# Shared expert of the last sequences moved behind the expert blocks, a wider ring of row numbers, and a new hand-written order in a one-core decoder layer

## The chip, the core and the metric

The kernel runs on one core of a Trainium2 chip. The core has five engines with an instruction stream each: TensorE (PE; its weight loads are listed apart as PEld), VectorE (DVE), ScalarE (ACT), GpSimd (POOL) and SyncE (SP), which here only issues transfers. Each engine works through its own stream in order, and streams wait for each other by semaphores. Transfers run on 16 DMA engines. The metric is the device time of one launch in microseconds.

## The reference, cut to what matters

A pre-norm decoder layer on 16 sequences of 256 tokens with 256 features, all in f32: attention with 16 heads of 16 features, an additive "cross" term, and a mixture of 16 experts with one shared expert. `ln` is a layer norm.

```python
# attention, after ln twice (the second with weight and bias)
q, k, v = heads(h @ w_q), heads(h @ w_k), heads(h @ w_v)        # rope on q and k
t = 1 + s + 0.5 * s * s            # s = q k^T / 4, a Taylor softmax
x = x + ((t / t.sum(-1)) @ v) @ w_o
# cross: a number per token plus a number per feature column
x = x + (ln(x) @ w_dec)[:, :, None] + (ctx @ w_enc)[:, None, :] + bias
# experts, y = ln(x)
scores = sigmoid(y @ gate_w.T)
topk_w, topk_idx = top_k(scores, 2)              # normalised, times 2.5
routed = sum over the two chosen e of weight * (silu(y @ w_gate[e]) * (y @ w_up[e])) @ w_down[e]
shared = (silu(y @ ws_gate) * (y @ ws_up)) @ ws_down
x = x + routed + shared
```

## The kernel before, in words

**Two phases.** In the first, the 16 sequences go through attention, cross term and routing. In the second, the routed expert work is done in 79 blocks of 128 rows, each block of one expert.

**First phase.** A `Sequence` has some 50 small tasks as methods (`turn_h`, `project`, `rope`, `score`, `square`, `product`, `output`, `decode`, `choose`, `place`, `enlist` and so on), and each task issues the instructions of one engine, mostly. The list `ORDER` (L854) is an order written out by hand: iteration i of the loop at L906 walks it once, and an entry (lag, task) runs that task for sequence i - lag. So tasks of up to eight sequences alternate in each engine's stream; the largest lag is 7, and the loop runs for 16 + 7 iterations. The last iterations, in which there are no new sequences, hold less and less of this work. A sequence ends with its routing: `logits` and `sigmoid` give scores, `choose` takes the top two on VectorE, `count` and `place` work out a row number ("slot") for each choice of a token, and `enlist` (L791) writes each token's normalised row with its weights to these slots of a DRAM table `listed`, in four indirect transfers that POOL issues. Every tile in PSUM of this phase comes from three pools: `p_sc` (two buffers, scores), `p_av` (one) and `p_t` (three, everything else).

**Shared expert.** `Shared` (L809) treats four token tiles (512 tokens) as a unit; there are eight units. `gate_up` is eight TensorE instructions into a `p_sc` buffer, `hidden` is a sigmoid on ACT and two multiplications on VectorE, `down(half)` is four TensorE instructions into a `p_t` buffer, and `add(half)` adds two token tiles to `x_all` on VectorE. The list `DRAIN` (L873) puts these pieces among the entries of the last iterations: (3, 24, 0, "down", 0) runs `down(0)` of unit 0 before entry 24 in iteration 16 + 3. What is left runs after the last iteration.

**Second phase.** `Block` i loads 128 rows of `listed` on SP (nine blocks ahead; the first load waits for all enlistings), `turn` transposes them on TensorE and ACT copies them, `pick` works out on VectorE each row's weight and its row number in the result, an i32 column `dest` from a ring of six buffers (L959), `hidden_product` multiplies by the block's expert (`gu`) and takes Silu on ACT, `weigh` multiplies on VectorE, `turn_hidden` transposes (`th`, copied to `hidT` on VectorE), and `give` (L996) multiplies by the down weights (`eo`), copies to `got` (ACT, six buffers) and writes the rows to a DRAM table `given` at `dest` by an indirect transfer from POOL. Step i of the loop at L1049 runs these stages for blocks i, i - 2, i - 3 and i - 4.

**Sums.** All rows of sequence b are given once block `last`(b) is. At step `last` + 7 `fetch(b)` (L1015) reads the two rows of each of its tokens back on SP, 512 KB, and waits for every `give` issued so far that no earlier fetch has waited for:

```python
ins = nc.sync.dma_start(out=got, in_=given_t[:, ts(b, TT)])
behind(ins, gave)
gave.clear()
```

From four steps later on, one `add` (L1025) a step adds a part of 128 x 256 to `x_all`, and the fourth writes the sequence out on SP:

```python
nc.vector.tensor_tensor(acc, acc, got[:, t, c], ALU.add)
if part == 2 * TT - 1:
    nc.sync.dma_start(out=out_t[:, ts(b, TT)], in_=x_all[:, ts(b, TT)])
```

What has not been added when the loop ends is added behind it (L1079).

Of the kernel before, what the change touches and what calls it, by code (L numbers as in the profile page):

```python
# [51 lines left out]
P = 128  # L52
# [23 lines left out]
def decoder_kernel(  # L76
# [192 lines left out]
    with tc.tile_pool(name="work", bufs=2) as work, tc.tile_pool(  # L269
# [576 lines left out]
        def turn_gate():  # L846
# [5 lines left out]


        ORDER = [  # L854
            (3, "score", 1), (4, "turn_x", 1), (3, "square", 1, 0), (7, "enlist", 1),
            (2, "rope", 1), (4, "normalise", 0), (5, "turn_h3"), (4, "normalise", 1),
            (3, "product", 0), (5, "copy_h3"), (5, "logits"), (0, "load"), (0, "stat"),
            (3, "square", 1, 1), (4, "turn_w"), (0, "experts", 0), (5, "sigmoid"), (1, "turn_h"),
            (1, "encode"), (4, "copy_w"), (5, "choose"), (2, "rope_sum", 1), (1, "copy_h"),
            (3, "score", 2), (4, "output"), (3, "square", 2, 1), (2, "turn_q"), (3, "sum_values"),  # L860
            (4, "add_y"), (3, "square", 2, 0), (3, "copy_vsum"), (3, "turn_vsum"),
            (3, "product", 1), (4, "decode"), (3, "score", 3), (6, "enlist", 0), (2, "copy_q"),
            (2, "turn_k"), (3, "copy_x", 0), (0, "scale"), (5, "count"), (3, "square", 3, 0),
            (1, "project_v"), (4, "scale_dec"), (3, "square", 3, 1), (0, "norm"),
            (3, "product", 2), (2, "copy_k", 0), (0, "experts", 1), (4, "get_enc"), (5, "place"),
            (3, "product", 3), (2, "copy_k", 1), (2, "score", 0), (4, "add_cross"),
            (1, "project", 0), (1, "rope", 0), (4, "norm3"), (3, "copy_x", 1), (1, "copy_v"),
            (1, "rope_sum", 0), (1, "project", 1), (2, "square", 0, 1), (2, "square", 0, 0),
            (3, "turn_x", 0),
        ]  # L870


        DRAIN = [  # L873
            (2, 50, 3, "gate_up"), (2, 62, 0, "gate_up"), (3, 4, 3, "hidden"), (3, 9, 0, "hidden"),
            (3, 24, 0, "down", 0), (3, 30, 0, "add", 0), (3, 35, 5, "gate_up"),
            (3, 47, 3, "down", 1), (3, 49, 3, "down", 0), (3, 51, 5, "hidden"),
            (3, 53, 6, "gate_up"), (3, 54, 1, "gate_up"), (3, 59, 3, "add", 0),
            (3, 60, 3, "add", 1), (3, 61, 6, "hidden"), (3, 64, 5, "down", 0), (4, 5, 5, "add", 0),
            (4, 7, 1, "hidden"), (4, 10, 0, "down", 1), (4, 12, 6, "down", 0),
            (4, 20, 0, "add", 1), (4, 21, 7, "gate_up"), (4, 23, 6, "add", 0),  # L880
            (4, 25, 1, "down", 0), (4, 31, 7, "hidden"), (4, 44, 4, "gate_up"),
            (4, 46, 1, "add", 0), (4, 57, 5, "down", 1), (4, 58, 5, "add", 1),
            (4, 60, 6, "down", 1), (4, 61, 2, "gate_up"), (5, 24, 7, "down", 0),
            (5, 26, 4, "hidden"), (5, 30, 6, "add", 1), (5, 44, 4, "down", 0),
            (5, 45, 2, "hidden"), (5, 50, 4, "down", 1), (5, 63, 7, "add", 0), (6, 9, 4, "add", 0),
            (6, 12, 4, "add", 1), (6, 18, 2, "down", 0), (6, 32, 1, "down", 1),
            (7, 9, 2, "add", 0), (7, 21, 2, "down", 1), (7, 27, 7, "down", 1),
            (7, 33, 2, "add", 1), (7, 38, 7, "add", 1), (7, 57, 1, "add", 1),
        ]
        first = Sequence(0)  # L890
        first.stat()
# [35 lines left out]
    with tc.tile_pool(name="ew", bufs=3) as ew, tc.tile_pool(  # L927
# [12 lines left out]
        class Block:  # L940
# [14 lines left out]
            def pick(self):  # L955

                code, own = self.rows[:, D + 2 : D + 3], codes[:, self.i : self.i + 1]
                self.weight = ew.tile([P, 1], F32, tag="weight", name="weight", bufs=4)
                self.dest = ew.tile([P, 1], I32, tag="dest", name="dest", bufs=6)  # L959
                nc.vector.scalar_tensor_tensor(  # L960
                    self.weight, code, own, self.rows[:, D : D + 1], ALU.is_equal, ALU.mult
                )
                nc.vector.scalar_tensor_tensor(
                    self.dest, code, own, self.rows[:, D + 3 : D + 4], ALU.is_equal, ALU.add
                )

                nc.vector.tensor_tensor(
                    self.weight, self.weight, self.rows[:, D + 1 : D + 2], ALU.max
                )
# [26 lines left out]
            def give(self):  # L996
                eo = p_e.tile([P, D], F32, tag="eo", name="eo")
                nc.tensor.matmul(  # L998
                    eo, lhsT=self.hidT,
                    rhs=wd_sb[:, ds(self.e, 1)].rearrange("m a d -> m (a d)"),  # L1000
                    start=True, stop=True,
                )
                got = ew.tile([P, D], F32, tag="got", name="got", bufs=6)
                nc.scalar.copy(got, eo)  # L1004
                ins = nc.gpsimd.indirect_dma_start(  # L1005
                    out=given,
                    out_offset=bass.IndirectOffsetOnAxis(
                        ap=self.dest, axis=0
                    ),
                    in_=got, in_offset=None,  # L1010
                    bounds_check=2 * NT * P - 1, oob_is_err=False,
                )
                gave.append(apart(ins, "given"))

        def fetch(b):  # L1015

            got = ew.tile([P, TT, 2, D], F32, tag="sum", name="sum")
            ins = nc.sync.dma_start(out=got, in_=given_t[:, ts(b, TT)])

            tc.add_to_no_dep_group("given", ins.ins)  # L1020
            behind(ins, gave)
            gave.clear()
            return got

        def add(b, got, part):  # L1025

            t, c = divmod(part, 2)
            acc = x_all[:, b * TT + t]
            nc.vector.tensor_tensor(acc, acc, got[:, t, c], ALU.add)
            if part == 2 * TT - 1:  # L1030
                nc.sync.dma_start(out=out_t[:, ts(b, TT)], in_=x_all[:, ts(b, TT)])

        AHEAD, LANDED, FETCHED = 9, 3, 4
        due = {}
        for b in range(B):
            last = min(NB, ((b + 1) * 2 * TT * P + E * (P - 1)) // P) - 1
            step = last + 4 + LANDED  # L1040
            if due:
                step = max(step, max(due) + 1)
            due[step] = b
# [2 lines left out]
        codes = block_codes()  # L1046
        blocks = [Block(i) for i in range(AHEAD)]
        expert, adds = [], []
        for i in range(max(due) + 1):  # L1049

            if i < NB and i % 4 == 0:
# [8 lines left out]
                blocks[i - 2].hidden_product(expert[i - 2])  # L1060
            if 3 <= i < NB + 3:
                blocks[i - 3].turn_hidden()
            if 4 <= i < NB + 4:
                blocks[i - 4].give()
            if i < NB:
# [10 lines left out]
                    adds.append((i + FETCHED + part, due[i], got, part))  # L1076
            if i + AHEAD < NB:
                blocks.append(Block(i + AHEAD))
        for _, b, got, part in adds:  # L1079
            add(b, got, part)  # L1080
        order.close()


# [30 lines left out]
```

## Time and profile before

| what | us |
|---|---|
| median of 3 runs (548.63 to 550.35) | 549.69 |
| the profiled execution | 552.59 |
| its span, first to last instruction | 550.8 |
| `gate_up` of all shared units on TensorE, 64 instructions, mean 598 ns | 29.2 busy |
| `down` of all shared units, 64 instructions, mean 385 ns | 15.7 busy |
| `given` writes, 79 issues by POOL, mean 987 ns | 78.0 busy |
| sums added on VectorE, 64 instructions, mean 420 ns | 26.6 busy |

Times in a trace are counted from the first instruction of the profiled execution. A row of instructions names line, engine and operation, what it writes and reads, and how often; "busy" is its time in total. TensorE work is pipelined, so its instructions overlap: eight pieces of `gate_up` take 3.43 us in the chain of work, though each lasts 0.6. Idle time before a group is put down to the instruction whose end released it. The chain of work that ended last is followed back from the last instruction.

The first block of the second phase has its rows transposed at 392.96 us, the last `gu` starts at 534.42, and the last indirect write leaves POOL at 539.23.

### The profile page before, as it was taken

The numbers are of one execution on the slowest core, as the hardware profiler recorded it, in microseconds if no ns is written. First come the engines' busy times: TensorE is split into PE (matmuls) and PEld (weight loads), VectorE is DVE, ScalarE is ACT, GpSimd is POOL, SyncE is SP. The second block draws the span as 40 slices with busy tenths as digits, with TensorE's granted clock in tenths as the row PEclk, the third lists the DMA queues.
The fourth block names the chain that finished last, engine by engine and source line by source line (L and its number), as shares of the span: only waits on it lengthen the run. The fifth ranks groups of instructions, "written<-read, shape, count | busy, mean of one in ns | idle before, by whom it ended". The sixth has DMA issues, their size and how long they took to land.

```text
span 550.8 us, 13145 instructions
## 1 busy us (share of the span) xinstructions
PE 506.6 (92%) x4299; PEld 348.0 (63%) x4299; DVE 400.5 (73%) x1723; ACT 307.6 (56%) x651; POOL 309.3 (56%) x496
## 2 busy tenths in 40 slices
PE   2899999999999999999999988999799999889880
PEld 1455676676666666667667654556588878677760
DVE  6534588899988989888888767898555566566663
ACT  3276686676676686676677674211255545445440
POOL 5743556577668668668665643544056555555541
PEclk9799999999999999999999999999899999999996
DMA  6974741241342242232001101101555377777734
GB/s 184 292 239 135 235 151 47 86 146 55 95 145 74 83 135 84 84 99 69 21 32 52 51 21 36 45 29 69 168 163 160 107 252 233 269 258 216 218 110 162
DMA packets 62066, 70.36 MB, mean 128 GB/s; under 512 B 7452, under 2 KB 53421, under 8 KB 62000
## 3 DMA queue, kind: packets, MB, share of 16 engines
q1 hardware_dynamic: 54592, 51.69, 31.0%
q0 software_dynamic: 6864, 17.06, 8.5%
q8 instruction: 35, 0.57, 0.4%
q10 hardware_dynamic: 544, 0.79, 0.4%
q14 instruction: 31, 0.25, 0.2%
HBM read 37.57 MB, written 33.89 MB: 130 GB/s over the span
## 4 chain that ended last, share of the span: by engine, by line
PE 78%; DMA 9%; DVE 5%; ACT 3%; issue 2%; POOL 2%; SPq 0%; POOLq 0%; ACTq 0%; DVEq 0%
PE sc L554 11%; PE av L574 10%; PE pq L458 10%; PE gu L975 8%; DMA given<-got,dest 7%; PE py L627 6%; PE pv L506 5%; PE shared_ps L818 5%; PE eo L998 4%; PE tp_h L438 3%; PE xt_ps L599 3%; PE shared_eo L834 2%; PE tp_e L951 2%; PE tp_k L438 2%; DMA sum<-given 2%
## 5 line engine op out<-in xcount | busy, mean ns | idle before, releaser
L564 ACT ACTIVATE a<-sc 128x1024 f32<-128x1024 f32 x128 | 126.3, 1034 | 52.3 <-PE sc L554 49.8
L1005 POOL DMA_INDIRECT given<-got,dest x79 | 78.0, 987 | 78.3 <-ACT rowsT L953 71.2
L975 PE MATMUL gu<-wgu_sb,rowsT 128*128 x316 | 83.1, 386 | 0.6 <-ACT rowsT L953 0.3
L793 POOL DMA_INDIRECT listed<-h,slots x64 | 65.3, 1021 | 20.7 <-issue 20.4
L554 PE MATMUL sc<-qT,kT 32*128 32x256 f32 x1024 | 76.0, 402 | 0.8 <-ACT a L564 0.8
L289 POOL TENSOR_SCALAR rs<-mv 128x2 f32<-128x2 f32 x48 | 11.5, 240 | 98.1 <-DVE mv L283 96.8
L574 PE MATMUL av<-a,vaug 128*32 128x256 f32 x1024 | 65.4, 382 | 0.0
L554 PEld LDWEIGHTS sc<-qT,kT 32*128 32x128 f32 x1024 | 48.2, 185 | 21.7 <-issue 12.7
L458 PE MATMUL pq<-wqkv,hT 128*128 128x512 f32 x128 | 59.1, 604 | 0.0
L975 PEld LDWEIGHTS gu<-wgu_sb,rowsT 128*128 128x128 f32 x316 | 54.7, 193 | 5.7 <-ACT rowsT L953 0.6
L290 POOL TENSOR_TENSOR rs<-rs,neg_half 128x2 f32<-128x2 f32 x64 | 48.8, 763 | 5.3
L480 POOL TENSOR_TENSOR qkr<-rot,m 128x512 f32<-128x512 f32 x32 | 41.1, 1286 | 16.1 <-DVE m L474 15.8
L1004 ACT COPY got<-eo 128x256 f32<-128x256 f32 x79 | 29.4, 373 | 34.1 <-PE eo L998 21.8
L998 PE MATMUL eo<-wd_sb,hidT 128*128 x158 | 47.7, 383 | 0.0
L574 PEld LDWEIGHTS av<-a,vaug 128*32 128x32 f32 x1024 | 29.0, 109 | 21.9 <-issue 4.9
L585 ACT ACTIVATE xs<-av,vsum 128x256 f32<-128x256 f32 x64 | 26.9, 471 | 27.5 <-PE av L574 20.6
L994 DVE COPY hidT<-th 128x128 f32<-128x128 f32 x79 | 22.7, 288 | 26.1 <-PE th L992 20.7
L981 ACT ACTIVATE hid<-gu 128x128 f32<-128x128 f32 x79 | 22.0, 278 | 35.1 <-PE gu L975 18.0
L468 DVE TENSOR_TENSOR rot<-pq,cosf 128x512 f32<-128x512 f32 x32 | 22.0, 686 | 26.3 <-PE pq L458 25.9
L458 PEld LDWEIGHTS pq<-wqkv,hT 128*128 128x128 f32 x128 | 23.1, 189 | 28.0 <-issue 24.4
L282 DVE BATCH_NORM_STATS2 st<-x_all 128x6 f32<-128x256 f32 x96 | 38.5, 401 | 2.7 <-DMA x_all<-in_x_dram 2.7
L298 POOL TENSOR_SCALAR h<-x_all,neg,rs 128x256 f32<-128x256 f32 x64 | 35.6, 561 | 3.4
(170 smaller groups left out, 1012.5 us busy)
## 6 DMA issues: line engine op xcount, KB each, us to landing
block<-listed SPq DMA_DIRECT2D x79, 132.0 KB
listed<-empty SPq DMA_DIRECT2D x9, 1056.0 KB
sum<-given SPq DMA_DIRECT2D x16, 512.0 KB
x_all<-in_x_dram SPq DMA_DIRECT2D x16, 256.0 KB
c<-in_ctx_dram SPq DMA_DIRECT2D x16, 256.0 KB
out_dram<-x_all SPq DMA_DIRECT2D x16, 256.0 KB
enc_row<-enc_rows SPq DMA_DIRECT2D x16, 128.0 KB
wgu_sb<-in_L_ffn_w_gate_dram SPq DMA_DIRECT2D x16, 128.0 KB
```

Source lines behind the costliest of these rows:

```text
L282: nc.vector.bn_stats(st, src[:, t])
L290: nc.gpsimd.tensor_tensor(r, r, neg_half, ALU.pow)
L298: nc.gpsimd.tensor_scalar(h[:, t, 0:D], src[:, t], neg[:, t : t + 1], r[:, t : t + 1], ALU.add, ALU.mult)
L458: nc.tensor.matmul(pq.rearrange("p h i two -> p (h i two)"), lhsT=self.hT[:, k, ts(t, P)], rhs=wqkv[:, k, 0 : 2 * D], start=(k == 0), stop ...
L480: nc.gpsimd.tensor_tensor(self.qkr[:, t], self.rot[t].rearrange("p h d -> p (h d)"), self.m2[t].rearrange("p h i two -> p (h i two)"), ALU ...
L554: nc.tensor.matmul(scs[j // 2][:, j % 2, kt], lhsT=self.kT[rows, g % 2, g // 2, ts(kt, P)], rhs=self.qT[rows, g // 2], start=True, stop=True,)
L564: nc.scalar.activation(a, self.scs[g][i], AF.Square, bias=1.0, scale=HD**-0.5)
L574: nc.tensor.matmul(self.av[ts(j, 32), g % 2], lhsT=self.va[:, kt, head], rhs=self.a[g, j // 2][:, j % 2, kt], start=(kt == 0), stop=(kt == ...
L793: ins = nc.gpsimd.indirect_dma_start(out=listed, out_offset=bass.IndirectOffsetOnAxis(ap=self.slots[:, i, t : t + 1], axis=0), in_=self.h3 ...
L975: nc.tensor.matmul(gu, lhsT=self.rowsT[:, k], rhs=wgu_sb[:, ds(e, 1), k].rearrange("p a i m -> p (a i m)"), start=(k == 0), stop=(k == KT ...
L998: nc.tensor.matmul(eo, lhsT=self.hidT, rhs=wd_sb[:, ds(self.e, 1)].rearrange("m a d -> m (a d)"), start=True, stop=True,)
L1005: ins = nc.gpsimd.indirect_dma_start(out=given, out_offset=bass.IndirectOffsetOnAxis(ap=self.dest, axis=0), in_=got, in_offset=None, bound ...
```

## The change

Six things are changed.

1. `ORDER` is a new list: the largest lag is 6 for 7, and tasks stand at other places and lags (for instance `project` at lag 2 for 1, the last two `product` at lag 4 for 3).
2. `DRAIN` is a new list with units 0 to 5 only.
3. The shared expert of sequences 12 to 15 is done by `SharedLate`, a sequence (256 tokens) each: `gate_up` with Silu on ACT in place of sigmoid and a multiplication, and `down` token tile by token tile. The first `gate_up` stands in step NB + 2 of the block loop, ahead of that step's `give`; the others behind the loop.
4. `dest` has 12 buffers for 6.
5. A fetch waits for the gives of blocks up to `last`(b) only, not for all issued so far.
6. The last sequence's fetch is split by token tile between the SP and ACT queues, and so is its output. A sequence's (or, for the last, a token tile's) output is issued once all additions to it are counted down (`added`).

```diff
         ORDER = [
-            (3, "score", 1), (4, "turn_x", 1), (3, "square", 1, 0), (7, "enlist", 1),
...
+            (2, "project", 0), (4, "product", 2), (0, "load"), (4, "product", 3), (3, "score", 0),
+            (4, "copy_x", 1), (2, "project", 1), (2, "rope", 0), (3, "square", 0, 1),
+            (4, "turn_x", 0), (3, "square", 0, 0), (3, "score", 1), (3, "square", 1, 1),
+            (2, "rope", 1), (2, "project_v"), (0, "experts", 0), (4, "normalise", 0),
+            (3, "square", 1, 0), (4, "turn_x", 1), (3, "turn_vsum"), (0, "stat"), (5, "turn_h3"),
+            (3, "product", 0), (4, "normalise", 1), (2, "copy_v"), (2, "rope_sum", 0),
+            (5, "copy_h3"), (5, "logits"), (1, "turn_h"), (5, "sigmoid"), (1, "encode"),
+            (4, "turn_w"), (5, "choose"), (2, "rope_sum", 1), (3, "score", 2), (4, "copy_w"),
+            (1, "copy_h"), (4, "output"), (3, "square", 2, 0), (6, "enlist", 0), (4, "add_y"),
+            (3, "square", 2, 1), (2, "turn_q"), (4, "get_enc"), (6, "enlist", 1),
+            (2, "sum_values"), (2, "copy_q"), (3, "product", 1), (0, "experts", 1),
+            (3, "score", 3), (4, "decode"), (0, "scale"), (5, "count"), (3, "copy_x", 0),
+            (4, "scale_dec"), (0, "norm"), (5, "place"), (2, "copy_vsum"), (4, "add_cross"),
+            (2, "turn_k"), (3, "square", 3, 0), (3, "square", 3, 1), (2, "copy_k", 0),
+            (4, "norm3"), (2, "copy_k", 1),
         ]
         DRAIN = [
...
+            (3, 2, 0, "gate_up"), (3, 7, 5, "gate_up"), (3, 12, 0, "hidden"), (3, 26, 5, "hidden"),
+            (3, 56, 3, "gate_up"), (3, 60, 0, "down", 0), (3, 60, 0, "add", 0),
+            (4, 0, 3, "hidden"), (4, 1, 5, "down", 0), (4, 1, 5, "add", 0), (4, 3, 0, "down", 1),
+            (4, 9, 0, "add", 1), (4, 9, 2, "gate_up"), (4, 23, 2, "hidden"), (4, 26, 3, "down", 0),
+            (4, 39, 3, "add", 0), (4, 43, 1, "gate_up"), (4, 54, 3, "down", 1),
+            (4, 58, 4, "gate_up"), (4, 64, 3, "add", 1), (5, 20, 2, "down", 0),
+            (5, 33, 1, "hidden"), (5, 55, 2, "add", 0), (5, 64, 5, "down", 1),
+            (6, 33, 5, "add", 1), (6, 38, 4, "hidden"), (6, 46, 1, "down", 0),
+            (6, 49, 1, "down", 1), (6, 64, 1, "add", 0), (7, 1, 1, "add", 1), (7, 5, 2, "down", 1),
+            (7, 19, 4, "down", 1), (7, 46, 2, "add", 1), (7, 50, 4, "down", 0),
+            (7, 50, 4, "add", 0), (7, 60, 4, "add", 1),
         ]
-                self.dest = ew.tile([P, 1], I32, tag="dest", name="dest", bufs=6)
+                self.dest = ew.tile([P, 1], I32, tag="dest", name="dest", bufs=12)
-                gave.append(apart(ins, "given"))
+                gave.append((self.i, apart(ins, "given")))
         def fetch(b):
             got = ew.tile([P, TT, 2, D], F32, tag="sum", name="sum")
-            ins = nc.sync.dma_start(out=got, in_=given_t[:, ts(b, TT)])
-            tc.add_to_no_dep_group("given", ins.ins)
-            behind(ins, gave)
-            gave.clear()
+            parts = [(nc.sync, ts(b, TT), got)]
+            if b == B - 1:
+                parts = [
+                    ((nc.sync, nc.scalar)[t], ds(b * TT + t, 1), got[:, ds(t, 1)]) for t in range(TT)
+                ]
+            for queue, tiles, part in parts:
+                ins = queue.dma_start(out=part, in_=given_t[:, tiles])
+                tc.add_to_no_dep_group("given", ins.ins)
+                behind(ins, [other for i, other in gave if i <= lasts[b]])
+            gave[:] = [g for g in gave if g[0] > lasts[b]]
             return got
+        def added(b, t):
+            left[b, t] -= 1
+            if b == B - 1 and left[b, t] == 0:
+                queue = (nc.sync, nc.scalar)[t]
+                queue.dma_start(out=out_t[:, b * TT + t], in_=x_all[:, b * TT + t])
+            elif b < B - 1 and not any(left[b, i] for i in range(TT)):
+                nc.sync.dma_start(out=out_t[:, ts(b, TT)], in_=x_all[:, ts(b, TT)])
         def add(b, got, part):
...
-            if part == 2 * TT - 1:
-                nc.sync.dma_start(out=out_t[:, ts(b, TT)], in_=x_all[:, ts(b, TT)])
+            added(b, t)
+        class SharedLate:
+            def gate_up(self):
+                ps = p_e.tile([P, 2, T], F32, tag="gu", name="late_ps")
+                for i in range(2):
+                    for k in range(KT):
+                        nc.tensor.matmul(
+                            ps[:, i], lhsT=wgu_sb[:, E, k, i], rhs=h3T[:, k, ts(self.b, T)],
+                            start=(k == 0), stop=(k == KT - 1),
+                        )
+                self.hid = ew.tile([P, T], F32, tag="late", name="late", bufs=4)
+                nc.scalar.activation(self.hid, ps[:, 0], AF.Silu)
+                nc.vector.tensor_tensor(self.hid, self.hid, ps[:, 1], ALU.mult)
+            def down(self):
+                for t in range(TT):
+                    eo = p_e.tile([P, D], F32, tag="eo", name="late_eo")
+                    nc.tensor.matmul(
+                        eo, lhsT=self.hid[:, ts(t, P)], rhs=wd_sb[:, E], start=True, stop=True,
+                    )
+                    acc = x_all[:, self.b * TT + t]
+                    nc.vector.tensor_tensor(acc, acc, eo, ALU.add)
+                    added(self.b, t)
+        LATE = 12
+        left = {(b, t): 2 + (b >= LATE) for b in range(B) for t in range(TT)}
...
+        late = [SharedLate(b) for b in range(LATE, B)]
...
                 blocks[i - 3].turn_hidden()
+            if i == NB + 2:
+                late[0].gate_up()
             if 4 <= i < NB + 4:
                 blocks[i - 4].give()
...
+        for n in range(1, len(late)):
+            late[n].gate_up()
+            if n > 1:
+                late[n - 2].down()
         for _, b, got, part in adds:
             add(b, got, part)
+        for other in late[-2:]:
+            other.down()
```

## The prediction

> **What bounds the kernel now.** I read the page first (busy time, 40 slices), then engine time by stage, then the waits, then the chain that ended last. The page's share of TensorE and its slices:
>
> ```profile
> PE 506.6 (92%) x4299; PEld 348.0 (63%) x4299; DVE 400.5 (73%) x1723; ACT 307.6 (56%) x651; POOL 309.3 (56%) x496
> ...
> PE   2899999999999999999999988999799999889880
> ```
>
> TensorE sets the time almost everywhere, so a gain must come from where this row is broken or from work taken off it where it is full. The stages, cut at the breaks (stage, length, busy PE, PEld, DVE, ACT, POOL, then granted clock, DMA share, GB/s):
>
> ```profile
> 23.90:300.00 276.10, 275.10 (x2929) 180.20 (x2928) 220.70 (x891) 192.47 (x343) 176.50 (x317) 0.99 0.35 108
> ...
> 339.00:374.00 35.00, 34.13 (x161) 19.41 (x160) 29.74 (x116) 6.52 (x13) 16.33 (x25) 1.00 0.11 39
> 374.00:389.20 15.20, 14.99 (x53) 9.53 (x52) 11.92 (x38) 1.19 (x2) 3.90 (x4) 1.00 0.12 44
> 389.20:394.00 4.80, 1.19 (x7) 0.77 (x7) 2.55 (x10) 0.47 (x2) 0.00 (x0) 0.94 0.70 200
> 394.00:442.00 48.00, 48.00 (x258) 40.48 (x259) 24.46 (x137) 27.52 (x87) 25.32 (x26) 0.97 0.52 163
> 442.00:535.00 93.00, 83.89 (x442) 66.92 (x441) 60.69 (x300) 45.32 (x148) 48.75 (x49) 1.00 0.68 220
> 535.00:551.00 16.00, 2.45 (x11) 1.17 (x9) 6.07 (x17) 1.40 (x4) 3.90 (x4) 0.66 0.49 164
> ```
>
> See four things. The steady loop is full (1.0 us idle of 276). From 339 to 389 the shared expert keeps TensorE full, so there its work costs its own length. The blocks run without a gap until 442 and lose over 9 us from then to 535. The last 16 us hold almost no TensorE work. Waits within 436 to 540, then the sync queue's own (waiter, releaser, total, times, longest):
>
> ```profile
> DVE dest L963 <- DMA given<-got,dest: 19.9, 17, 3.3
> ...
> DVE x_all L1029 <- DMA sum<-given: 3.2, 3, 1.3
> ```
>
> ```profile
> SPq L1018 <- DMA given<-got,dest: 56.8, 16, 12.6
> ...
> SPq L944 <- PE shared_eo L834: 4.4, 1, 4.4
> ```
>
> The 9 us follow from `dest`: VectorE waits for a buffer that an indirect write still reads, and `hidT` and `hid`, which TensorE needs, queue behind it. The last line says that the first block load waited for the shared expert's last product (389.1), not for the list. The end of the chain:
>
> ```profile
> 539.23 2.09 DMA given<-got,dest
> 541.32 0.02 issue
> 541.34 4.66 DMA sum<-given
> ...
> 547.28 0.42 DVE x_all L1029
> ```
>
> **1. Two of eight shared units leave the handover.** A unit is a gate_up of 3.43 us on TensorE (x8 pieces of the chain) and two downs of 0.87 (x8 in 1.73): 5.2 us; on VectorE 2.6 us (0.69 + 0.61 and two adds of 0.68, less overlap). Two units: 10.4 us off TensorE. If TensorE alone counted, the last product would end at 389.1 - 10.4 = 378.7. But the last sequence's list is then late: `count` ends at 373.8, the slots at 378.7, four enlistings start 1.28 apart from 379.13 to 382.97 and land 2.1 later (row 539.23), at 385.1; the first transpose of a block follows its release by 3.8 (389.14 to 392.96), at 388.9 instead of 392.96. So with the old deal the gain is 4 us, with TensorE alone 10.4. The new order (largest lag 6 for 7) and the new deal decide. I follow them by hand. Sequence work alone would have ended `count` at 373.8 - 27.7 (five gate_ups and seven downs before it) - 4.0 (gaps from 322 to 373) = 342.1. The new end of `turn_x` 0 of sequence 15 has 5.3 us of that still ahead of it, two gate_ups (6.9) inside it and about 2.6 us of gaps in the iteration before, where `score` 1 waits for two squares (1.94) behind 0.5 us of `turn_x`: 346.3. From there VectorE's order is the chain: to the end of `choose`(14) 6.0, `add_y` and `decode` 2.7, `place`(14) 3.85, `add_cross` 1.95 (sum 14.5); POOL's norm 2.4; transposes, one down, logits and sigmoid 2.2; `choose` 3.4; an add and `place` to the slots 4.0; three enlist steps 3.9 and landing 2.1: 32.5. The shared rest, twelve downs and four gate_ups dealt behind it and paced by VectorE's adds, ends at about 34.2. First block product at 346.3 + 34.2 + 3.8 = 384.3 for 392.96: **-8.7**, ends -4 and -11.
>
> **2. Twelve `dest` buffers.** Gives 1 to 27 come every 1.627 us; the 52 steps to the last take 539.23 - 442.29 = 96.9 for 84.6: 12.3 lost. With six, `dest` of block i waits for give i-6, issued two steps (3.3 us) earlier; a landing takes 3.9 to 6.2 us here (chain pieces 511.56, 519.46). With twelve it has eight steps. What is late next is `got` with its unchanged six buffers: six steps, 9.8 us against 6.2, so hidden; if landings grew past 9.8 it would take over. TensorE's gaps that do not follow a `dest` wait (463.4, 487.8, 491.6) sum to about 1.5. **-11**, ends -6 and -12.5.
>
> **3. A fetch waits only for the blocks that it needs.** Now it waits for gives issued up to its own step; then only for those issued three steps (4.9 us) earlier. The sums come sooner, which removes what is left of the 3.2 us of sum waits, mostly inside 2. Own value 0. Block loads behind it on SP are nine ahead and gain only slack.
>
> **4. The tail.** Count from the start of the last `gu` (534.42): the end is at 16.4. In the new order late gate_up 0 stands between the last transpose and the last two gives. At 256 columns it costs 1.81 (row `pv` x8). The last give leaves POOL at about 6.1 for 4.8 and lands at 8.2. Then the fetch in halves on SP and ACT. Here a rule speaks against the change: the Trainium skill (DMA: Bandwidth & Descriptors, "Issuing engines are not separate DMA queues") has all queues share the same 16 engines, so a second one saves only issue time. The row: 512 KB took 4.66 us with the previous fetch in flight, 3.61 (482.09) without; an issue on SP takes 0.37. Halving by queues would give 2.3, the rule 3.3 to 3.6. I take 3.6, since the previous fetch now leaves earlier: sums at 11.8. ACT now issues a half. SP, in the trace, stood up to 12.6 us with such a wait and issued nothing meanwhile; so I have ACT stand until 8.3, and the Silus of late 1 to 3 stand behind it. So late gate_up 3, which needs the `gu` buffer of late 1, starts at 9.5 and ends at 11.3; its mul ends at 12.2; late 1's adds at 13.1; seven sum adds of 0.40 at 15.9; four late adds, the last two paced by `eo` buffers (0.5 us of product each), at 17.8. Behind the last add the trace has 3.1 us (547.7 to 550.8). End at 20.9: **+4.5**. Ends: 0 if the late work hid wholly (a give later by 1.3, a fetch shorter by 1.1), +7 if ACT's wait delays every late step in turn.
>
> **5. The order in the steady loop and at the start.** The same TensorE work per iteration, 20.05 us. Nothing says that it can't be packed: the tightest place is `score` 1 behind `score` 0: two squares end 3.2 after `score` 0 starts, and 1.08 + 1.77 + 0.53 = 3.4 of TensorE work stands between. VectorE has 17.7 of 20 and POOL 14; every p_t buffer is free in my count before its third successor. At the start, the first query transpose waits for the same `qkr` sums (22.4), since POOL norms sequence 1 before them. **0**, ends -2 and +4 (0.25 per iteration). Leaving `Shared` 6 and 7 out frees memory only: 0.
>
> **Sum.** -8.7 - 11 + 4.5 = -15.2 on a profiled execution of 552.6 (span 550.8), which is 2.9 above the median of the runs, 549.69. I put the difference on the median: **534.5 us**.
>
> **Rivals.**
> A, the transfers take over from the buffers (20%). For: a steady step moves 132 KB of block, 128 given, 128 fetched and 64 written: 452 KB of 1,024 bytes, which at 1.63 us is 284 GB/s, and the busiest 19.5 us stretch (461.5 to 481) has 275 at a share of 0.77. Against: the start moved 292 GB/s. If landings stretch so that `got` or the sums hold VectorE, half of the 11 us stays: 540.
> B, the list decides the handover (14%). VectorE is busy 29.7 of 35 us there, and each shared add and mul stands in its queue ahead of `place`. Then only the 4 us come: 539.
> C, slower (12%): the new order stalls the loop. One mechanism: `score` 1 waiting for the squares of `score` 0, whose slack is 0.2 us; anything that holds ACT for longer (`copy_x` 1 now stands directly ahead of them, 0.84 us) stops TensorE in each of some 14 iterations. It decides from 15.2 / 14 = 1.1 us per iteration. At 1.5 us: 549.7 - 15.2 + 21 = 555. Against: `copy_x` 1 fits beside `score` 0 (1.08), and in the old order ACT kept up with less than 15 us of work in 20.
> D, the parts don't do what they say: `gave` was cleared at each fetch and may have hidden a wait that is simply moved; its price is inside A.
>
> **From these to the numbers.** Forecast 53%, A 20%, B 14%, C 12%, no change 1%. Adding the ends of 1, 2, 4 and 5 as independent gives about 6 us either way around 534.5; the upper end reaches past A and B: 527 to 544. Under 0.3% (1.6 us), about what a measurement of this kernel can tell from no change, lie 2%. Faster 0.86, same 0.02, slower 0.12.
>
> **What would show it.** 1: first transpose of a block near 384 for 392.96, TensorE full to about 380. 2: gives every 1.63 us to the end and no `dest` wait on DMA. 3: the sync queue's wait for gives down from 56.8. 4: from the last `gu` to the end 20 to 21 us for 16.4, with ACT's first late Silu behind the last give's landing. 5: 20.1 us from one iteration to the next. I am wrong if `score` shows new waits for `a` in the loop, if `got` waits for DMA, or if the tail alone is longer by over 7.

## The result, and the profile after

The changed kernel took 599.38 us (median of 4 runs, 595.96 to 601.94), and the kernel before, beside it on the same chip, 550.02. The ratio is 1.091, 95% interval 1.087 to 1.095: slower by 49 us where 15 us less was forecast. The profiled execution took 601.94, with a span of 600.2. Here and below, an execution more than 1.5% above the fastest of its kernel is left out of medians and ratios.

Two rows of the changed kernel's page, in 40 slices of 15 us:

```profile
PE   3899998898898987989889898889889999989894
...
PEclk9799999998987989889888898989989999999898
```

TensorE is no longer full from slice 7 to slice 30, which is the loop over the sequences with its last iterations, and its clock falls there too. From one `output` to the next the loop takes 24.6 us for 20.1 before (mean of eight iterations). The first block transpose comes at 436.7 for 392.96, so 44 of the 49 us are lost in the first phase. From there to the last `gu` it takes 139.1 us for 141.5, and from that `gu` to the end 24.3 for 16.4.

The waits of the changed kernel from 100 to 340 us (waiter, releaser, total, times, longest) show where the loop stands:

```profile
ACT sT L683 <- PE sc L554: 29.5, 9, 3.6
...
PE py L627 <- ACT wvT L621: 24.9, 10, 3.1
```

In each of ten iterations TensorE stands 2.5 us on average ahead of `output` until ScalarE has copied `wvT`. In ScalarE's stream that copy stands behind the sigmoid of `logits`, which waits too. `a`, which rival C named, shows no such wait. The timeline of one iteration follows, with the rows of GpSimd, TensorE and ScalarE that matter (start, length, what ran, in brackets the idle time ahead of it). `pl` is what `logits` writes, `tp_w` what `turn_w`, `sc` what `score`, `py` what `output`; `sT` is written by `sigmoid`, `wvT` by `copy_w`, and the four rows that write `listed` are `enlist`:

```profile
281.83 1.11 POOL L793 DMA_INDIRECT listed<-h,slots  x1 [0.16 <-issue]
...
283.04 0.41 PE L676 MATMUL pl<-h3T,gateT 128*32 128x64 f32 x16
283.24 0.97 POOL L793 DMA_INDIRECT listed<-h,slots  x1 [0.30 <-issue]
...
283.87 0.60 PE L438 MATMUL tp_w<-ident,wv 128*128 128x128 f32 x4
...
284.40 1.34 PE L554 MATMUL sc<-qT,kT 32*128 32x256 f32 x16
284.52 0.97 POOL L793 DMA_INDIRECT listed<-h,slots  x1 [0.30 <-issue]
...
285.79 0.98 POOL L793 DMA_INDIRECT listed<-h,slots  x1 [0.30 <-issue]
286.04 0.22 ACT L683 ACTIVATE sT<-pl 128x64 f32<-128x64 f32 x1 [3.20 <-PE sc L554]
...
287.52 0.58 ACT L621 COPY wvT<-tp_w 128x512 f32<-128x512 f32 x1 [1.26 <-remote]
...
288.16 0.80 PE L627 MATMUL py<-wo_sb,wvT 128*128 128x256 f32 x1 [2.42 <-ACT wvT L621]
```

`pl`, the result of `logits`, ends at 283.45 by its records, but the sigmoid that reads it starts at 286.04. The count by which TensorE tells the other engines that it has finished goes up at 286.02, 2.57 us after `pl`. The counts for `tp_w` and for both halves of `sc`, which had ended by 285.74, follow only at 287.50, 287.63 and 287.69. So TensorE's records end, and the other engines see its completions late. From 281.83 to 286.77 GpSimd issues the four indirect writes of `enlist`, 0.30 us apart. After 2.4 us of idle TensorE also runs slowly. The same iteration in windows (length, busy PE, PEld, DVE, ACT, POOL, then granted clock, DMA share, GB/s):

```profile
282.90:286.00 3.10, 2.84 (x48) 2.12 (x40) 0.64 (x3) 0.00 (x0) 2.19 (x4) 1.00 0.26 95
286.00:288.20 2.20, 0.04 (x1) 0.04 (x1) 1.63 (x9) 0.90 (x3) 1.89 (x4) 0.86 0.70 221
288.20:291.60 3.40, 3.40 (x11) 2.76 (x12) 1.41 (x10) 2.84 (x6) 1.31 (x4) 0.59 0.14 51
```

At a clock of 0.59 the eight pieces of `output` take 3.4 us; they take 2.0 in the undisturbed run below. Idle time and slow pieces make 3.8 of the some 4.5 us that an iteration lost.

### The profile page after: what moved, and what is told of

Read it like the earlier page. It is cut to its first block, busy times and chain, and to the rows that moved or that the text cites. A ratio compares the mean times of both kernels' runs of the same rounds, so it can differ in the third digit from the quotient of the medians.

```text
span 600.2 us, 13157 instructions
## 1 busy us (share of the span) xinstructions
PE 533.2 (89%) x4315; PEld 366.2 (61%) x4315; DVE 391.6 (65%) x1727; ACT 311.2 (52%) x653; POOL 310.3 (52%) x496
## 4 chain that ended last, share of the span: by engine, by line
PE 77%; DVE 7%; DMA 5%; another core or an unknown queue 3%; issue 3%; POOL 2%; ACT 2%; SPq 0%; POOLq 0%
PE sc L554 12%; PE gu L971 10%; PE av L574 10%; PE pq L458 9%; PE py L627 8%; PE eo L994 5%; PE pv L506 5%; PE tp_e L947 3%; PE tp_h L438 2%; DMA given<-got,dest 2%; PE xt_ps L599 2%; DMA sum<-given 2%; PE tp_q L438 2%; PE th L988 1%
## 5 line engine op out<-in xcount | busy, mean ns | idle before, releaser
L564 ACT ACTIVATE a<-sc 128x1024 f32<-128x1024 f32 x128 | 124.2, 1024 | 35.1 <-PE sc L554 33.8
L971 PE MATMUL gu<-wgu_sb,rowsT 128*128 x316 | 84.5, 391 | 0.4 <-ACT rowsT L949 0.4
L793 POOL DMA_INDIRECT listed<-h,slots x64 | 64.5, 1007 | 23.6 <-issue 23.0
L627 PE MATMUL py<-wo_sb,wvT 128*128 128x256 f32 x128 | 47.0, 531 | 31.5 <-ACT wvT L621 24.9
L574 PE MATMUL av<-a,vaug 128*32 128x256 f32 x1024 | 66.9, 390 | 0.0
L458 PE MATMUL pq<-wqkv,hT 128*128 128x512 f32 x128 | 64.7, 631 | 0.7 <-ACT hT L448 0.7
L627 PEld LDWEIGHTS py<-wo_sb,wvT 128*128 128x128 f32 x128 | 32.4, 266 | 43.4 <-ACT wvT L621 29.4
L977 ACT ACTIVATE hid<-gu 128x128 f32<-128x128 f32 x79 | 21.9, 278 | 36.9 <-PE gu L971 20.4
L1040 DVE TENSOR_TENSOR x_all<-x_all,sum 128x256 f32<-128x256 f32 x64 | 26.5, 420 | 20.9 <-DMA sum<-given 20.4
```

The lines of the kernel that those rows point to most:

```text
L458: nc.tensor.matmul(pq.rearrange("p h i two -> p (h i two)"), lhsT=self.hT[:, k, ts(t, P)], rhs=wqkv[:, k, 0 : 2 * D], start=(k == 0), stop ...
L564: nc.scalar.activation(a, self.scs[g][i], AF.Square, bias=1.0, scale=HD**-0.5)
L574: nc.tensor.matmul(self.av[ts(j, 32), g % 2], lhsT=self.va[:, kt, head], rhs=self.a[g, j // 2][:, j % 2, kt], start=(kt == 0), stop=(kt == ...
L627: nc.tensor.matmul(self.py[:, q], lhsT=self.wvT[:, k, ts(q, P)], rhs=wo_sb[:, k], start=(k == 0), stop=(k == KT - 1),)
L793: ins = nc.gpsimd.indirect_dma_start(out=listed, out_offset=bass.IndirectOffsetOnAxis(ap=self.slots[:, i, t : t + 1], axis=0), in_=self.h3 ...
L971: nc.tensor.matmul(gu, lhsT=self.rowsT[:, k], rhs=wgu_sb[:, ds(e, 1), k].rearrange("p a i m -> p (a i m)"), start=(k == 0), stop=(k == KT ...
```

## The experiments

The experiments ran on five chips (5, 0, 9, 14 and 12, in this order), each group of runs on one, and no chip was used twice. The chip of the result is not known. Which group a run belongs to turned out to matter more than any edit.

**The order alone, and the rest alone (chip 5).** `old_order` puts the old lists back into the changed kernel; `new_order_alone` puts the new ones into the kernel before:

```diff
-ORDER = [new];  DRAIN = [new]
+ORDER = [old];  DRAIN = [old without units 6 and 7]      # old_order
-ORDER = [old];  DRAIN = [old]
+ORDER = [new];  DRAIN = [new, units 6 and 7 behind]      # new_order_alone
```

> The changed kernel with the old ORDER and the old DRAIN without units 6 and 7; all else of the change stays. Theory S (the loss is the new order's alone: in each iteration of the loop the output product waits for wvT): iterations of 20.1 us again and the first block transpose at 384 to 389. The rest of the change then shows its own worth. As the second phase of the changed kernel has it (2.3 us gained from the first transpose to the last gu, 8 lost behind it), the time is 547 to 552; as the prediction had it (-11 and +4.5), 534 to 539. Rival R (the other parts took more than 10 us of the 49): 560 or above.

> The kernel before with the new ORDER, and the new DRAIN with units 6 and 7 dealt behind the others; nothing else of the change. Theory S: the loop takes 24 to 25 us per iteration as in the changed kernel, and two units more stand ahead of the blocks (up to 10.4 us), so 594 to 604. Rival R: at most 575.

Measured beside 551.17: `old_order` 557.12, ratio 1.011 (1.006 to 1.016), 20.07 us per iteration; `new_order_alone` 613.53, ratio 1.115 (1.106 to 1.124), 25.1 us per iteration. The last is 10 us above its window, with the iterations as expected. On this chip the loss in the loop comes with the new order. But the rest of the change gains nothing either: 557 is above both its windows.

**What in the order (chip 5).**

```diff
-... (5, "logits"), ... (4, "output"), (3, "square", 2, 0), ...
+... (4, "output"), (5, "logits"), (3, "square", 2, 0), (5, "sigmoid"), ... (4, "add_y"), (5, "choose")   # logits_later
-(1, "turn_h"), ... (4, "turn_w")
+(4, "turn_w"), ... (1, "turn_h")                                                                          # turn_w_first
```

> The changed kernel with logits behind output on TensorE, sigmoid behind the first square of score 2 on ScalarE and choose behind add_y on VectorE. Theory S (the completion of logits comes late to ScalarE, and copy_w stands behind the sigmoid that waits for it): output waits under 0.5 us, iterations of 20 to 21 us, 555 to 565 in all. Rival K (copy_w is late for another reason, or the clock is low in this order anyway): output still waits over 2 us, 24 us per iteration, 590 or more.

> The changed kernel with turn_w and turn_h changed over, so that TensorE has logits, turn_w, turn_h, score 2, output as before the change. Theory S: nothing much changes, 24 us per iteration, 595 to 602, since the completion of logits is as late. Rival T (what stands directly behind logits sets when its completion is seen): 20.5 us per iteration, about 555.

`logits_later` 595.73 (1.079, 1.074 to 1.084), 23.2 us per iteration; `turn_w_first` 600.74 (1.093, 1.084 to 1.103), 24.7. In `logits_later` the wait ahead of `output` is gone, as theory S says, but the completion of `logits` is still seen 1.6 us late, and now `ps_vsum` waits for the sigmoid (1.5 us), `ahead` for VectorE and `pv` too. So theory S named the victim and not the cause. What goes on while completions are late is GpSimd's four writes back to back. The old order issues them in two pairs, some 1.5 us apart, and there (the trace of before) the delay is 0.9 and 1.65 us in turns.

**Moving the writes (chips 0, 9 and 14, then 12).** `enlist_behind_norm` moves both enlist entries of the new order behind `norm`, `enlists_together` joins the two of the old order:

```diff
-(4, "output"), (3, "square", 2, 0), (6, "enlist", 0), ... (6, "enlist", 1), ... (0, "norm"), (5, "place")
+(4, "output"), (3, "square", 2, 0), ... (0, "norm"), (6, "enlist", 0), (6, "enlist", 1), (5, "place")   # enlist_behind_norm
-(7, "enlist", 1), ... (6, "enlist", 0)
+(7, "enlist", 1), (7, "enlist", 0), ...                                                                 # enlists_together
```

> The changed kernel with its two enlist entries moved behind norm of the next sequence, so that GpSimd issues the four indirect writes some 10 us after logits and not around it. Theory E (while GpSimd issues indirect writes back to back, TensorE's completions of logits and of what follows reach the other engines late): the completion of logits is seen within 0.1 us of its end, output waits under 0.5 us, 20 to 20.8 us per iteration, 552 to 562 in all. Rival P (logits itself or the lower clock makes them late): still 2.5 us late, 24 us per iteration, 590 or more.

> The kernel before with its second enlist moved directly behind the first, at the head of the iteration, so that four indirect writes follow each other around logits as in the changed kernel; nothing else. Theory E: the completion of logits comes 2.5 us or more late for 0.9 to 1.7 before, output waits 1.5 to 3 us in each of some 13 iterations, 575 to 600 in all. Rival P: 0.9 to 1.7 us late as before, 549 to 553.

On chip 0, beside 547.72: 550.8 (1.007, 1.004 to 1.009) and 557.64 (1.018, 1.015 to 1.021). The first looked like the cure. The second contradicted it: its four writes stand around `logits`, and yet its completion is seen 0.19 us late at most in the loop. (It loses 0.7 us per iteration, of which its trace shows 0.55: from 100 to 310 us TensorE waits ten times, 5.5 us in all, for `qkr`, GpSimd's sum of the rotated queries and keys. `dest12`, with the old order, has no such wait.) The kernels with the old order on this chip also show 0.04 to 0.18 us, with the same writes around `logits` as in the trace of before. So what differed was the chip, or something else that differs from group to group, and the changed kernel itself was run again:

> The changed kernel once more, beside enlist_behind_norm_2 on one chip, since the kernels of the last four runs showed the completion of logits 0.04 to 0.19 us behind its end where the runs ahead of them showed 0.5 to 1.7 with the same instructions around it. Theory E (held completions make the loss of the loop): where the completion is seen over 2 us late, 24 us per iteration and about 599; where it is seen within 0.2 us, 20 us per iteration and about 552. Rival Q (the order itself costs 4 us per iteration): 24 us per iteration in either case.

> The kernel enlist_behind_norm again, beside the changed kernel on one chip. Theory E: within 1% of 550.8 whatever after_again does. Rival Q2 (it was quick since that chip holds no completion back): as slow as after_again.

> The kernel enlists_together again. Theory E: if after_again shows completions of logits over 2 us late, so does this one, with output waiting in each iteration, 575 to 600; if not, 557 as before.

On chip 9, beside 547.22, the changed kernel takes 547.24, ratio 0.9995 (0.997 to 1.002). `enlist_behind_norm_2` takes 548.9 (1.004, 1.001 to 1.006) and `enlists_together_2` 554.22 (1.013, 1.007 to 1.019). The page and the timeline of that run of the changed kernel:

```profile
PE   2899999999999999999999999887999988989884
...
PEclk9899999999999999999999999999899999989997
```

```profile
248.79 1.11 POOL L793 DMA_INDIRECT listed<-h,slots  x1 [0.16 <-issue]
...
249.93 0.41 PE L676 MATMUL pl<-h3T,gateT 128*32 128x64 f32 x16
...
250.21 0.97 POOL L793 DMA_INDIRECT listed<-h,slots  x1 [0.31 <-issue]
...
250.41 0.22 ACT L683 ACTIVATE sT<-pl 128x64 f32<-128x64 f32 x1 [0.68 <-PE pl L676]
...
251.40 0.58 ACT L621 COPY wvT<-tp_w 128x512 f32<-128x512 f32 x1 [0.76 <-PE tp_w L438]
...
252.37 1.99 PE L627 MATMUL py<-wo_sb,wvT 128*128 128x256 f32 x8
```

It is the same program with the same writes around the same products, but the sigmoid starts 0.07 us after `pl`, and an iteration takes 19.90 us. The groups after it were to set the two side by side on a chip with late completions:

> The changed kernel a third time, beside enlist_behind_norm_3. Theory E: 599 where the completion of logits is seen over 2 us late, 547 where it is seen within 0.2 us; nothing between. Rival Q: a time between these with completions in time.

> The kernel enlist_behind_norm a third time. Theory E: 546 to 556 also where after_third takes 599, since no indirect write is issued around logits. Rival C2 (on such a chip TensorE's completions come late wherever they are): 580 or more beside a changed kernel of 599. Where after_third takes 547, this run tells nothing between the two.

> The changed kernel once more, beside enlist_behind_norm_4. Theory E: 599 where the completion of logits is seen over 2 us late, 547 where it is seen within 0.2 us.

> The kernel enlist_behind_norm once more. Theory E: 546 to 556 also where after_fourth takes 599. Rival C2: 580 or more beside a changed kernel of 599. Where after_fourth takes 547, it tells nothing between the two.

On chip 14 completions came in time: beside 546.97 the two took 546.66 (0.999, 0.996 to 1.002) and 549.15 (1.005, 1.003 to 1.008). On chip 12 they came late: beside 550.25 the changed kernel took 596.19 (1.083, 1.080 to 1.087), and `enlist_behind_norm_4` 596.9 in the quicker of two runs. So theory E's cure fails. Rival C2 has the time right, but not for its reason, since completions are not late wherever they are: with the writes away from `logits`, `pl` is seen 0.04 us after its end in each iteration of the loop, and what now stands beside the writes is seen late. A timeline of `late_ahead_of_sums` (below), which has the same order on the same chip:

```profile
222.57 1.93 PE L574 MATMUL av<-a,vaug 128*32 128x256 f32 x32
...
222.76 1.11 POOL L793 DMA_INDIRECT listed<-h,slots  x1 [0.17 <-issue]
...
226.73 0.97 POOL L793 DMA_INDIRECT listed<-h,slots  x1 [0.30 <-issue]
...
227.03 0.84 ACT L585 ACTIVATE xs<-av,vsum 128x256 f32<-128x256 f32 x2 [3.95 <-PE sc L554]
```

`av`, what `product` writes, ends at 224.51, its completion is seen at 227.01, and `copy_x` (the row of `xs`) starts then; the other two of the four writes stand between the two shown. On chip 14 the same `copy_x` started 0.06 us after `av`. In `after_fourth`, on the same chip 12 but with the writes around `logits`, `av` is seen 0.04 us after its end all through the loop, and `pl` 2.6 to 4.5. So on such a chip the delay follows the writes.

The same can be counted over whole traces. Take the instructions of ScalarE and VectorE that a completion of TensorE released. Of those whose product ended during an `enlist` write or just beside it, 26 of 57 started more than 1 us after that end in the changed kernel (4.6 at most), 8 of 36 in the kernel before (1.9 at most), and none of 59 in `after_again` (0.23 at most). Away from the writes it is none of 120 in the changed kernel (0.10 at most), and beside the writes of the second phase, which mostly stand 0.65 us apart, 1 of 103.

All profiled runs but that of `enlist_behind_norm_4` (its trace is of the run of 608.2), sorted by chip and by how the writes of an iteration stand (us from one `output` to the next, mean of eight iterations):

| | four writes back to back | two pairs |
|---|---|---|
| completions late (the result's chip, 5, 12) | 24.6, 24.5 (changed kernel), 25.1, 24.7, 23.2, 24.5 (`late_ahead_of_sums`) | 20.08 (before), 20.07 |
| completions in time (0, 9, 14) | 19.90 (changed kernel and all with the new order), 20.62 (`enlists_together`) | 19.88 |

In these runs the loss comes only where both meet: a chip on which completions come late, and four writes in a row.

**The second phase (chips 0, 9, 14, 12).** `dest12` gives the kernel before 12 buffers of `dest` and nothing else; `late_dest6` is `old_order` with 6 again:

```diff
-self.dest = ew.tile([P, 1], I32, tag="dest", name="dest", bufs=6)
+self.dest = ew.tile([P, 1], I32, tag="dest", name="dest", bufs=12)     # dest12; late_dest6 the other way
```

> The kernel before with 12 buffers of dest, nothing else. By the prediction's step 2: -11, so 539. Theory D (adds that wait for a sum's transfer stand in VectorE's queue and take the place of the dest waits): the waits of DVE for sum grow from 7.9 us to 15 or more, the last gu starts at most 4 us earlier, 546 to 550.

> The kernel old_order (557.1) with 6 buffers of dest again, so that what is left of the change is the late shared expert, the narrower waits of the fetches and the two queues at the end. By the prediction's step 2: 568. Theory D: 557 to 561, with the dest waits back and the sum waits gone.

`dest12` 544.57, ratio 0.994 (0.991 to 0.997): 3 us instead of 11. `late_dest6` 554.93, 1.016 (1.010 to 1.021), with 25.3 us of `dest` waits and 9.2 of sum waits: the late shared units, with the fetches and queues that go with them, cost 7 us there. The waits of `dest12` from 390 us on, and two pieces of its chain:

```profile
DVE x_all L1029 <- DMA sum<-given: 23.6, 15, 4.6
```

```profile
450.16 5.51 DMA given<-got,dest
455.73 4.11 DMA sum<-given
```

The adds of a sum stand in VectorE's queue four steps (6.5 us) behind their fetch, which itself waits for a write to land: 5.5 and 4.1 us here. VectorE stops at the first add, and `hidT` and `hid` queue behind it, as they did behind `dest`. The cure is one number:

```diff
-AHEAD, LANDED, FETCHED = 9, 3, 4
+AHEAD, LANDED, FETCHED = 9, 3, 7
```

> The kernel before with 12 buffers of dest and the sums added from 7 steps behind their fetch instead of 4. Theory D (with dest out of the way the adds that wait for a sum's transfer stop VectorE, 23.6 us in dest12): the waits for sum within the loop fall under 5 us, the last gu starts 3 to 6 us earlier than in dest12 counted from the first transpose, ratio to before about 0.985. Rival W (the transfers themselves set the pace of the second phase): the waits move to got or to block loads, and the time is that of dest12, ratio 0.994.

> enlist_behind_norm with the sums added from 7 steps behind their fetch instead of 4. Theory D: as in dest12_adds_later the waits for sum within the blocks go, the last gu starts at 129 to 132 us behind the first transpose for 137.9, 540 to 544 in all (ratio near 0.985); the late shared units keep the end 6 to 8 us longer than in dest12_adds_later (536.1). Rival W: the late units and the sums collide behind the last block, and the end grows past 28 us.

`dest12_adds_later` (before, 12 buffers, adds three steps later) takes 536.08 beside 547.22, ratio 0.980 (0.973 to 0.986), and beats both kernels on that chip. Later adds with six buffers were not tried. From the first transpose to the last `gu` it takes 129.6 us for 136.5 in `dest12`, and its waits from 390 us on have left of this row:

```profile
DVE x_all L1029 <- DMA sum<-given: 5.0, 3, 4.5
```

`moved_adds_later`, the same in `enlist_behind_norm`, takes 540.16, 0.989 (0.982 to 0.996), with 129.1 us for these steps.

**The end (chip 12).** `late_ahead_of_sums` is `moved_adds_later` with the last fetch and output on SP alone and the late units ahead of the adds:

```diff
-    parts = [((nc.sync, nc.scalar)[t], ds(b * TT + t, 1), got[:, ds(t, 1)]) for t in range(TT)]
...
+for other in late[-2:]: other.down()
 for _, b, got, part in adds: add(b, got, part)
-for other in late[-2:]: other.down()
```

> moved_adds_later (540.2) with the last fetch and output whole on SP's queue and all late shared work ahead of the adds behind the loop, so that neither the Silus on ScalarE nor the late multiplications on VectorE stand behind a wait for the last give or the last sum. Theory L (these two waits make the 23 us from the last gu to the end): 16 to 19 us from the last gu to the end, 532 to 536 in all. Rival M (the late work itself is too long for the time in which the last rows are written and read back): 22 us or more, 539 to 541.

It ran on a chip with late completions: 591.92, 1.075 (1.070 to 1.080), 4.3 below the changed kernel there. Its end, counted from the last `gu`, is 21.9 us long, for 23.0 in `after_fourth` on the same chip and 23.6 in `moved_adds_later`. That is close to rival M's 22, though the waits went: VectorE's sum adds, 4.1 us, now stand behind the late ones and end last.

## Why the prediction was wrong

**Step 5, the order in the loop (0, ends -2 and +4; measured about +54 on the result's chip).** This is the step that failed. From the first `output` to the first block transpose the changed kernel takes 381.9 us there, for 328.0 in `after_again` and `after_third`; against the kernel before, with 338.8, it loses 43 in spite of step 1. I counted engine work and buffers per iteration and found that 20 us of work can be packed, which is right: 19.90 us where completions come in time. What I left out is that the new list also moves the four writes of an iteration from two pairs to four in a row, and that TensorE's completions can be seen late beside them. I priced no part of `enlist`, though each of its issues takes 1 us on GpSimd. On a chip like the result's, products that end beside them are seen up to 4.6 us late, the sigmoid and `copy_w` with it start late, and `output` waits. The trace of before had the clue, in its waits from 80 to 300 us:

```profile
ACT sT L683 <- PE tp_h L438: 7.3, 6, 1.4
```

The sigmoid reads `pl`, but is released after `tp_h`, a later product. Here a releaser that is not the producer says that the completion came late (`pl` is seen 0.9 and 1.65 us after its end in turns), while GpSimd issued a pair of writes. It cost nothing there, because `output` was not yet due. I did not read that row.

**Rival C (555).** Right in kind (the order stalls the loop, in each iteration) and wrong in place and price: not `score` 1 behind its squares, but `output` behind `copy_w`, 4.5 us and not 1.5. Where completions come in time it does not come true at all.

**Step 1 (-8.7).** About right where the loop is undisturbed. From the first `output` to the first block transpose, `after_again` and `after_third` take 328.0 us, `dest12` with the old first phase 335.2: -7.2. With the old order and two units fewer (`late_dest6`) it is 334.4, so nearly all of it comes from the new order and deal; the 4 us that the step gave to the old deal are 0.8.

**Step 2 (-11).** The cover was named wrongly. I put `got` next behind `dest` and found it hidden; next were the sum adds, 23.6 us of waits. The 11 us are there, once the adds stand later: `dest12_adds_later` is 11.1 below the kernel before on chip 9, and its steps take 129.6, for 139.5 in `enlists_together_2` on the same chip, whose second phase is that of before (142.6 in `enlists_together` on chip 0, so such a figure is good to some 3 us). Rival A had this half right: the sums do hold VectorE, but by the distance at which the adds stand, not because transfers fill the engines.

**Step 3 (0, sum waits gone).** Wrong from its premise on: the fetches don't leave earlier. Sequence 14 is complete with block 74, whose `give` GpSimd issues at 520.69 in `after_again`. From the chain of that run:

```profile
526.43 2.09 DMA given<-got,dest
...
528.71 3.48 DMA sum<-given
```

The write of 526.43 is the last but one of 79, that of block 77, and the fetch that follows is that of sequence 14. It is so throughout: before the change and after it, a fetch is released by the landing of the `give` three blocks after `last` (13 fetches in the trace of before, 13 in that of the changed kernel and 15 in `after_again`; the last fetch has no later `give`, and for the others the traces name no releaser). So the fifth part of the change, the narrower wait, does not show in the traces, and why it does not stays open. Rival D had asked whether the parts do what they say. The sync queue's wait for gives, 56.8 before, hardly moved; from 437 us on in the changed kernel:

```profile
SPq L1020 <- DMA given<-got,dest: 52.0, 17, 6.5
```

With the adds at a fixed four steps behind such a fetch, a `dest` that no longer slows the blocks only brings the adds forward. The waits for sums did not go but grew, from 7.9 us in the second phase before to 20.4.

**Step 4 (+4.5, ends 0 and +7; measured +8).** This is over the 7 that the prediction had named as a sign of being wrong. ScalarE's stand came as forecast, but a wait of VectorE was left out. In the timeline of `after_again` the last `gu` starts at 521.47, and then:

```profile
530.26 0.35 ACTq L1020 DMA_DIRECT2D sum<-given  x1
530.66 0.66 ACT L1059 ACTIVATE late<-late_ps 128x256 f32<-128x256 f32 x2 [4.07 <-PE late_eo L1065]
532.21 0.43 DVE L1040 TENSOR_TENSOR x_all<-x_all,sum 128x256 f32<-128x256 f32 x1 [4.44 <-DMA sum<-given]
532.56 0.74 DVE L1060 TENSOR_TENSOR late<-late,late_ps 128x256 f32<-128x256 f32 x2
...
533.02 3.57 PE L1054 MATMUL late_ps<-h3T,wgu_sb 128*128 128x256 f32 x8 [2.53 <-DVE late L1060]
```

The late Silus stand behind ScalarE's half of the last fetch until 530.66 (9.2 after that `gu`, for 8.3 forecast). The late multiplications then queue behind the first add of sequence 14, which waits for the fetch of step 3; the prediction had that fetch leave earlier. So `gate_up` 3 starts 11.6 us after that `gu` and not 9.5, and takes 3.6 us and not 1.8, at a granted clock of 0.52 (533.0 to 536.4) behind an idle TensorE. It ends 3.8 later than forecast, and the end, 24.4, comes 3.5 later than my 20.9.

**The sum.** With step 5 at zero and completions in time, -7 at the handover and +8 at the end cancel, and the blocks gain next to nothing (139.6 us in `after_again`, 139.5 in `enlists_together_2` beside it): 547.24 against 547.22. So the forecast of 534.5 would have been wrong on those chips too, by steps 2, 3 and 4.

## What to carry to other kernels

When a hand-written order is changed, list the transfers that each engine issues as well as its work, and keep an eye on writes issued back to back. Read the waits for rows whose releaser is not the producer: the completion may have come late, hidden only by slack. When a wait is made narrower, look in the trace whether it ends earlier. When a buffer wait goes, look at what else stands in that engine's queue at a fixed distance behind a transfer, and set that distance anew in the same edit; and measure on more than one chip before a difference is put down to an edit.

## What was not expected of the hardware

In three of six groups of runs (the result's, and those on chips 5 and 12) TensorE's completions were seen up to 4.7 us late while GpSimd issued indirect writes in a row; on chips 0, 9 and 14 the same completions of `logits` were seen within 0.6 us, and in the changed kernel within 0.21. In the iterations shown above VectorE's and ScalarE's completions came in time. Why the groups differ, and what holds the completions, stays open. So does how much of the loss is due to four writes in a row and how much to an order with less slack: `logits_later` loses 3 us per iteration, though the completions counted above are seen 2.0 us late at most in its trace, for 1.9 in the kernel before, whose loop loses 0.2. The new order with its writes in two pairs was not tried on a chip of the late kind, nor was `enlists_together`; these two would be the clean pair of tests, and no version with the new order is shown to run well on both kinds of chip. `dest12_adds_later` keeps the old order's pairs, but was itself timed on chip 9 alone.

The other surprise is how little idle time slows TensorE. The Trainium skill (TensorE: Matmul & The Clock Gate, "Part 1: The HAM clock gate") puts the drop to half clock behind an idle window of about 3.4 us. Here 2.42 us without a product were enough. The mean granted clock is 0.86 over 286.00 to 288.20, so the drop comes within the wait, and 0.50 from 288.2 to 290.9. Five of the eight pieces of `output` there start 0.43 us apart, for 0.216 in `after_again`. The measurement decides: a wait of 2.4 us cost 3.8.
